# Four mixed layers on one core: GpSimd's share of the products with C, whose engine copies a bank, and where loads are issued

## The chip, the cores and the metric

The kernel runs on one core of a Trainium2 chip. A core has five engines with instruction queues of their own: TensorE (PE, with its weight loads shown as PEld), VectorE (DVE), ScalarE (ACT), GpSimd (POOL) and SyncE (SP), which here only issues transfers. Transfers run on 16 DMA engines. The metric is the device time of one execution in microseconds, the median of several runs; smaller is better.

## The reference

Eight images of 96 channels and 64 x 64 pixels pass through four layers, each with a residual and a group norm in front (32 groups of 3 channels):

```python
x = x + _L0_conv_ref(_gn(x), ...)   # selective scan over the 4096 pixels of an image
x = x + _L1_conv_ref(_gn(x), ...)   # Fourier layer
x = x + _L2_conv_ref(_gn(x), ...)   # sampled positions, then 4 scans over patches of 4 x 4
x = x + _L3_conv_ref(_gn(x), ...)   # deformable 3 x 3 convolution
```

The scans of the layers 0 and 2 are, for 192 channels d and 16 states n,

```python
hst = hst * jnp.exp(dt[..., None] * A) + (dt * ut)[..., None] * bt
y = jnp.einsum('bkdn,bkn->bkd', hst, ct)
```

Layer 1 takes a 2-D real Fourier transform of each image, gates it by a grouped 24 x 24 product with gelu and a soft threshold, transforms back, projects the channels, and normalises with the mean and variance over all eight images before a last gelu. So nothing of its end can be finished before the last image has been transformed. All is float32.

## The kernel before, in words

**Scans.** Layers 0 and 2 work in chunks of 512 pixels. A chunk's 192 channels are 12 groups of 16 channels x 8 states on 128 partitions, with two halves of the states side by side. `Slots` writes the order of work out by hand: in slot t (one group) each engine's queue gets the pieces of several groups at different stages. For a group at slot t these are: at t-4 SP loads `dd` (delta and delta times u, each repeated for 8 states: 512 KB); at t-2 POOL multiplies with B (L348, `dbu`); at t-1 ACT takes the exponentials into PSUM (L327, `ps_d`); at t DVE scans (L675 in layer 0, L1501 in layer 2) and, if the group is not `late`, multiplies with C (L358, two instructions); PE sums over the states (L366). If the group is `late`, the scan writes to SBUF, and POOL does the product with C in one instruction a slot later (L353). In layer 0 the third of each six groups is late, two a chunk, whatever the chunk. `dd` has 5 buffers, `dbu` 6, and each of the two PSUM tiles `ps_d` 2.

Other pieces are put into the same slots with `sl.at(slot, engine, function)`. Layer 0 has 12 slots a chunk and 96 an image (B0 is an image's first slot); the next image's `xn` comes in eight pieces (L535), one a slot from B0 - 84 on, its statistics at B0 - 74 + c (L541). POOL also has the sums of softplus and two gating products (L414 to L426, L722). Layer 2 has 48 slots a chunk (B); a chunk's input rows `xl` are loaded at B - 92 (L1185), normalised at B - 89 on ACT (L1190, `pad`), convolved on PE (L1213), sampled on POOL (L1292 to L1316).

**Layer 1.** Per image: `down` (12 banks: two products on PE, L808, then four copies of 64 x 256 into `tr`), `along` (L833, evicted on ACT, L837), `gate` (L858 to L865, ACT and DVE), statistics of the image before on DVE (L936), four `down` of the next image, `project` (L875, evicted on ACT as `pt`, L882, 13 copies), then twelve `back` (L894) with the other eight `down` and six `up` (L913) between them. The order is written out, too. All products use one rotation of eight PSUM banks. In `down` the copies of a bank go alternately to DVE (L822, partitions 0 to 63 of `tr`) and ACT (L824, the others).

**The seam.** After the last image `yr` is read back, its statistics are taken, and the scale and shift of the normalisation computed (L976 to L983). `between()` sets up the weights of layer 2 (`weights2`: loads, products on PE, L1084 to L1113). Then four images are finished here: load `x` (L993), gelu on `yr` (ACT, L1015), addition (DVE, L995), store (L996), statistics (L229). The other four are finished in 16 pieces inside layer 2 (loads L1011 and L1012, addition L1672, statistics L1674, store L1020), 5, 5 and 6 of them in three batches, loaded at the slots -92, -60 and -46. Here the order is left to a scheduler, but for the slots of layer 2. The buffers of the finishing `x`, and layer 2's pools, lie in memory that earlier pools held, and become free when these pools are done. SP issues its transfers in order, and waits in this order for buffers and data.

Of the kernel before, what the change touches and what calls it, by code (L numbers as in the profile page):

```python
# [18 lines left out]
CH = 96  # L19
# [475 lines left out]
def layer0(S, src, dst, st_in, st_out, images):  # L495
    tc, nc = S.tc, S.nc
    with ExitStack() as ctx:
# [27 lines left out]
        def image(b, B0):  # L525
            im = {}

            def load():
                im["xn"] = xn = new(fp, [CH, 3 + NP], "xn", bufs=2)
                nc.vector.memset(xn[:, 0:3], 0.0)  # L530
                im["bns"] = new(fp, [CH, NC, 6], "ibns", bufs=2)

            def piece(c):
                at = slice(3 + c * NW, 3 + (c + 1) * NW)
                return lambda: nc.sync.dma_start(  # L535
                    im["xn"][:, at], src[b][:, c * NW : (c + 1) * NW]
                )

            def stats(c):
                def run():  # L540
                    nc.vector.bn_stats(  # L541
                        im["bns"][:, c, :], im["xn"][:, 3 + c * NW : 3 + (c + 1) * NW]
                    )

                return run

            im["nm"] = new(fp, [CH, 1], f"nm{b}")
            def normal(c):
                def run():
                    x = im["xn"][:, 3 + c * NW : 3 + (c + 1) * NW]  # L550
                    nc.scalar.activation(
                        x, x, AF.Identity, bias=im["nm"], scale=st_in[:, b, 1:2]
                    )

                return run

            sl.at(B0 - 84, "sp", load)
            for c in range(NC):
                sl.at(B0 - 84 + c, "sp", piece(c))
                sl.at(B0 - 74 + c, "dve", stats(c))  # L560
            GroupStats(
                S, sl, B0 - 62, st_in[:, b, :], lambda: im["bns"], fp, psk, "ps_k", im["nm"]
            )
            for c, t in enumerate((-50, -49, -46, -45, -38, -37, -34, -33)):
                sl.at(B0 + t, "act", normal(c))
            im["obns"] = new(fp, [CH, NC, 6], f"obns{b}")
            return im

        def chunk(im, b, c, T):
# [103 lines left out]
            def scan_of(n):  # L673
                def scan(i, out, da, dbu):
                    nc.vector.tensor_tensor_scan(  # L675
                        out, da, dbu, carry[:, n + i : n + i + 1] if c else 0.0, ALU.mult, ALU.add
                    )

                return scan
# [8 lines left out]
            def y_of(h, g):  # L688
                def run():
                    if g == 0:  # L690
                        ch["y", h] = new(psy, [128, NW], "ps_y")
                    return ch["y", h][:HD, :], g == 0, g == NG - 1

                return run
# [15 lines left out]
            for h in range(2):  # L710
                for g in range(NG):
                    t, n = T + h * NG + g, 2 * (h * NG + g)
                    sl.groups[t] = Group(
                        n=g, a=acol[:, n : n + 2], steps=steps_of(h, g), b=lambda: ch["b"],
                        c=lambda: ch["c"], y=y_of(h, g), scan=scan_of(n), late=g == 2,
                    )
                    if c < NC - 1:
                        sl.at(t, "end", keep(t, n))
                sl.at(T + (h + 1) * NG + 1, "dve", skip(h))
# [46 lines left out]
def layer1(S, src, mid, dst, st_in, st_out, images, finish, between):  # L766
# [4 lines left out]
    with ExitStack() as ctx:  # L771
# [17 lines left out]
        with ctx1:  # L789
# [10 lines left out]
            def down(im, q):  # L800


                if q == 0:
                    im["tr"] = new(ip, [128, IH, CH], "tr")
                ps = ps_of()
                for r in range(2):
                    c0 = 4 * q + 2 * r
                    nc.tensor.matmul(  # L808
                        ps[:, r * 256 : (r + 1) * 256],
                        im["xh"][:, c0 : c0 + 2, :].rearrange("h c w -> h (c w)"),  # L810
                        fh,
                        start=True,
                        stop=True,
                    )
                to = im["tr"].rearrange("p k (s q r i) -> p q i r s k", s=2, r=2, i=2)
                for i in range(2):
                    for part in range(2):
                        o = to[part * 64 : part * 64 + 64, q, i]
                        v = ps[i * 64 : i * 64 + 64, :]
                        v = v.rearrange("p (r s q k) -> p q r s k", r=2, s=2, q=2)[:, part]  # L820
                        if part == 0:
                            nc.vector.tensor_copy(o, v)  # L822
                        else:
                            nc.scalar.copy(o, v)  # L824
# [156 lines left out]
        nc.vector.tensor_tensor(mv[:, 0:1], mv[:, 0:1], vec[:, 0:1], ALU.subtract)  # L981
        nc.vector.tensor_tensor(sc[:, 1:2], mv[:, 0:1], sc[:, 0:1], ALU.mult)
        nc.vector.tensor_tensor(sc[:, 1:2], vec[:, 2:3], sc[:, 1:2], ALU.subtract)  # L983
        between()
        with ExitStack() as ctx2:
            ip = ctx2.enter_context(tc.tile_pool(name="l1j", bufs=3))
            psp = ctx2.enter_context(tc.tile_pool(name="l1g", bufs=2, space=PSUM))

            here = list(kept)[-4:]
            for b in here:  # L990
                yb = kept[b]
                xb = new(ip, [CH, NP], "x2")
                nc.sync.dma_start(xb, src[b])  # L993
                finish.gelu(yb)
                nc.vector.tensor_tensor(xb, xb, yb, ALU.add)  # L995
                nc.sync.dma_start(dst[b], xb)  # L996
                S.image_stats(st_out[:, b, :], xb, wp, psp, "ps")
# [30 lines left out]
def weights2(S, cp):  # L1028

    tc, nc = S.tc, S.nc  # L1030
    with tc.tile_pool(name="l2s", bufs=4, space=PSUM) as psa:
# [34 lines left out]
        centre = new(cp, [HD, 2, HD], "centre")  # L1066
        nc.vector.tensor_tensor(centre[:, 0, :], S.ident[:HD, :HD], kmean, ALU.subtract)
        nc.vector.tensor_scalar(centre[:, 1, :], kmean, -1.0, None, ALU.mult)
        with tc.tile_pool(name="l2t", bufs=1) as tp:
            wx = S.load("l2_wx", tp)  # L1070
            off1 = S.load("l2_off1", tp).rearrange("e h k o -> e h (k o)")
            xp = S.load("l2_xp", tp)
            dtw = S.load("l2_dt", tp)
            ds = new(tp, [CH, 4, DI], "ds")
            nc.sync.dma_start(ds, S.ins["l2_d"].unsqueeze(0).to_broadcast([CH, 4, DI]))
            nc.vector.tensor_tensor(ds[:, 0:2], ds[:, 0:2], ds[:, 2:4], ALU.add)
            nc.vector.tensor_tensor(wds, ds[:, 0], ds[:, 1], ALU.add)
            nc.vector.tensor_tensor(wds, wds, win[:, :DI], ALU.mult)
            flat = woff.rearrange("c k o -> c (k o)")
            for n in range(4):  # L1080
                at = slice(432 * n, 432 * n + 432)
                ps = ps_of()
                for h in range(2):
                    nc.tensor.matmul(  # L1084
                        ps[:CH, :432], wx[:, h, :], off1[:, h, at], start=h == 0, stop=h == 1
                    )
                nc.scalar.copy(flat[:, at], ps[:CH, :432])
            xpm = new(tp, [CH, 1, 4 * (RK + 2 * NS)], "xpm")
            ps = ps_of()
            for h in range(2):  # L1090
                nc.tensor.matmul(
                    ps[:CH, : 4 * 38],
                    wx[:, h, :],
                    xp[:, h].rearrange("e k c -> e (k c)"),
                    start=h == 0,
                    stop=h == 1,
                )
            nc.vector.tensor_copy(xpm[:, 0, :], ps[:CH, : 4 * 38])
            for k in range(4):
                at = 38 * k + RK  # L1100
                for what in range(2):
                    replicate(
                        nc, rep_w[:, k, what], xpm[:, 0, at + what * NS : at + (what + 1) * NS]
                    )
                ps = ps_of()
                for h in range(2):
                    nc.tensor.matmul(
                        ps[:RK, :CH], xp[:, h, k, :RK], wx[:, h, :], start=h == 0, stop=h == 1
                    )
                low = new(tp, [RK, CH], f"low{k}")  # L1110
                nc.vector.tensor_copy(low, ps[:RK, :CH])
                ps = ps_of()
                nc.tensor.matmul(ps[:CH, :DI], low, dtw[:RK, k, :], start=True, stop=True)  # L1113
                m = ORDER.index(k)
                nc.vector.tensor_copy(wd[:CH, m, :], ps[:CH, :DI])
                nc.sync.dma_start(wd[CH : CH + 1, m], S.ins["l2_dt"][RK : RK + 1, k])
# [6 lines left out]
def layer2(S, src, dst, st_in, st_out, images, cp, W, ready, finish):  # L1123
# [3 lines left out]
    with ExitStack() as ctx:  # L1127
# [8 lines left out]
            )  # L1136
        )

        fp = ctx.enter_context(tc.tile_pool(name="l2f", bufs=1))
        wp = ctx.enter_context(tc.tile_pool(name="l2w", bufs=1))  # L1140
        sl = Slots(S, cp, wp, psd)
        log_exp_tables(S)
        acol = sl.negative_exp("l2_alog")
# [33 lines left out]
        def front(ch, b, pad, xs, c, B):  # L1177
# [21 lines left out]
                r = 0 if c == 0 else 9  # L1199
                nc.gpsimd.memset(pad[:, r, :], 0.0)  # L1200

            sl.at(B - 92, "sp", load)
            sl.at(B - 89, "act", normal)
            if c in (0, NC - 1):
                sl.at(B - 89, "pool", border)
# [945 lines left out]
```

## Time and profile before

| | |
|---|---|
| median of 3 timed runs | 17438.37 us (17433.97 to 17443.99) |
| the profiled execution | 18287.47 us, its span 18285.7 us, mean granted clock 0.900 |
| busy share of the span | PE 78%, PEld 29%, DVE 89%, ACT 56%, POOL 84% |
| first scan instructions of layer 2 | 3961.71 us |
| last scan product of layer 2 | about 14454 us |
| HBM read and written | 579.53 MB and 87.69 MB |

The profiled execution is some 850 us longer than the timed ones, so a time from the trace is compared with other times of the trace. In the page, the busy share of an engine counts instructions that compute; a line of the groups gives the line in the kernel, engine, operation, output and inputs with their shapes, the count, the summed busy time, the mean duration in ns, and after the second bar the idle time just ahead of them with what ended it. A timeline row has start and length in us, and in brackets the idle time before it and its releaser. A row of the chain of waits has start, length and what was waited for or worked on. The windows view gives busy time per engine in stretches of the span.

### The profile page before, as it was taken

The page shows a single profiled execution, that of the slowest core. Times are in us where ns is not written, and L with a number is a line of the kernel's source. Part 1 is how long each engine was busy: PE and PEld are TensorE (multiplying, and loading weights), DVE is VectorE, ACT ScalarE, POOL GpSimd, SP SyncE. Part 2 cuts the span into 40 slices and gives each one's busy share as a digit, 9 for nine tenths or more (in the row PEclk, how much of TensorE's full clock was granted, in tenths as well). Part 3 has the DMA queues.
Part 4 walks back from the last instruction along what each step waited for, and adds up shares of the span by engine and source line. Part 5 has one row for each costly group of instructions (what it writes and reads, how often), then busy time and mean ns, then how long its engine had stood idle before and what let it go on. Part 6 is the DMA issues. An engine that isn't in the chain of part 4 may idle for free.

```text
span 18285.7 us, 141860 instructions
## 1 busy us (share of the span) xinstructions
PE 14310.8 (78%) x34756; PEld 5304.7 (29%) x34756; DVE 16268.6 (89%) x16810; ACT 10307.5 (56%) x17016; POOL 15303.1 (84%) x9100
## 2 busy tenths in 40 slices
PE   8999998858888888898898988889888644434333
PEld 2323334723333333333333333333333211111111
DVE  7999997559999999999999999999999766767667
ACT  6777775546666666766666666676666411111100
POOL 7999995049999999999999999999999656656555
PEclk8999998879999999999999999999999866666666
DMA  7888886269999999999999999999999745444444
GB/s 128 151 153 151 151 151 107 56 139 157 158 158 158 158 158 157 159 157 158 158 157 159 157 159 158 158 158 158 158 157 158 139 127 152 143 136 144 135 129 120
DMA packets 941060, 2689.99 MB, mean 147 GB/s; under 512 B 274482, under 2 KB 276223, under 8 KB 938605
## 3 DMA queue, kind: packets, MB, share of 16 engines
q1 hardware_dynamic: 792781, 2227.79, 70.0%
q0 software_dynamic: 147456, 453.13, 8.4%
q8 instruction: 284, 4.65, 0.1%
q14 instruction: 539, 4.42, 0.1%
HBM read 579.53 MB, written 87.69 MB: 36 GB/s over the span
## 4 chain that ended last, share of the span: by engine, by line
POOL 21%; PE 21%; issue 20%; DVE 18%; another core or an unknown queue 11%; ACT 5%; DMA 4%; SPq 0%; POOLq 0%; DVEq 0%; ACTq 0%
POOL dbu L348 12%; PE ps_y L366 9%; DVE ps_d L1501 7%; DVE dbu L358 6%; DMA dd<-delta 3%; POOL dbu L353 2%; PE ps_k L577 2%; PE ps_a L1820 2%; POOL sp_m L1435 1%; POOL delta L1443 1%; PE ps_o L2054 1%; DVE ps_d L675 1%; POOL sp_w L1438 1%; PE ps_k L1213 1%
## 5 line engine op out<-in xcount | busy, mean ns | idle before, releaser
L348 POOL TENSOR_TENSOR dbu<-dd,brep 128x1024 f32<-128x1024 f32 x3840 | 9062.4, 2376 | 187.8 <-DMA dd<-delta 127.2
L366 PE MATMUL ps_y<-dbu,k_red 128*96 128x512 f32 x15360 | 7447.2, 612 | 817.3 <-DVE dbu L358 496.5
L1501 DVE TENSOR_TENSOR_SCAN ps_d<-ps_d,dbu 128x512 f32<-128x512 f32 x5760 | 6710.3, 1208 | 83.7 <-POOL dbu L348 68.9
L327 ACT ACTIVATE ps_d<-dd,l_alog 128x512 f32<-128x512 f32 x7680 | 4991.7, 681 | 2708.3 <-DVE dbu L358 2571.5
L358 DVE TENSOR_TENSOR dbu<-ps_d,crep 128x512 f32<-128x512 f32 x7040 | 4437.1, 668 | 0.0
L366 PEld LDWEIGHTS ps_y<-dbu,k_red 128*96 128x96 f32 x15360 | 2407.3, 166 | 5459.1 <-issue 3158.6
L1985 POOL DMA_INDIRECT v<-t,idx x2304 | 2185.7, 949 | 1570.1 <-DVE s L2012 730.7
L2012 DVE TENSOR_REDUCE s<-v 128x864 f32<-128x3456 f32 x256 | 1554.2, 6071 | 369.7 <-remote 314.9
L2003 DVE TENSOR_TENSOR v<-v,ps_w 128x3456 f32<-128x3456 f32 x256 | 958.4, 3744 | 735.3 <-ACT ps_w L1995 658.4
L675 DVE TENSOR_TENSOR_SCAN ps_d<-ps_d,carry,dbu 128x512 f32<-128x512 f32 x1120 | 1373.4, 1271 | 80.9 <-POOL dbu L348 50.5
L2031 ACT COPY smp<-ps_t 128x768 f32<-128x768 f32 (+1 forms) x512 | 244.4, 529 | 1793.3 <-remote 1197.4
L1213 PE MATMUL ps_k<-pad,woff 96*96 96x512 f32 x2304 | 1093.8, 597 | 69.4 <-ACT pad L1190 66.9
L1480 PE MATMUL ps_a<-xs,rep_w 96*128 96x512 f32 x2048 | 1097.9, 617 | 53.3 <-ACT brep L1488 51.9
L2023 PE MATMUL ps_t<-k_ident,s 128*128 128x128 f32 (+1 forms) x1792 | 328.3, 334 | 1014.8 <-issue 695.1
L353 POOL TENSOR_TENSOR dbu<-h,crep 128x1024 f32<-128x1024 f32 x320 | 755.7, 2362 | 126.1 <-DVE h L1501 126.1
L1820 PE MATMUL ps_a<-xpad,l_om 96*27 96x512 f32 x1152 | 594.7, 667 | 22.5 <-issue 22.5
L1837 PE MATMUL ps_u<-k_ident,oc 27*128 27x27 f32 x256 | 33.0, 252 | 740.0 <-ACT oc L1832 666.8
L2023 PEld LDWEIGHTS ps_t<-k_ident,s 128*128 128x128 f32 (+1 forms) x1792 | 251.6, 170 | 1149.0 <-issue 985.1
L1213 PEld LDWEIGHTS ps_k<-pad,woff 96*96 96x96 f32 x2304 | 372.1, 164 | 708.9 <-issue 583.1
L1162 POOL MEMSET pad<- 96x660 f32 x4 | 2.4, 648 | 683.1 <-DMA y<-yb 683.1
L1435 POOL TENSOR_TENSOR sp_m<-sp_m,sp_s 128x512 f32<-128x512 f32 x384 | 495.4, 1290 | 59.1 <-ACT sp_s L1423 59.1
L1480 PEld LDWEIGHTS ps_a<-xs,rep_w 96*128 96x128 f32 x2048 | 347.1, 189 | 665.0 <-ACT brep L1488 286.2
(268 smaller groups left out, 17180.5 us busy)
## 6 DMA issues: line engine op xcount, KB each, us to landing
dd<-delta SPq DMA_DIRECT2D x3840, 512.0 KB
v<-t,idx POOLq DMA_INDIRECT x2304
xo<-x SPq DMA_DIRECT2D x128, 192.0 KB
x<-xo SPq DMA_DIRECT2D x128, 192.0 KB
xn<-x SPq DMA_DIRECT2D x64, 192.0 KB
xh<-x SPq DMA_DIRECT2D x16, 768.0 KB
y<-yb SPq DMA_DIRECT2D x16, 768.0 KB
yr<-y SPq DMA_DIRECT2D x8, 1536.0 KB
```

The lines of the kernel that those rows point to most:

```text
L327: nc.scalar.activation(da, g.dd[:, 0, :], AF.Exp, scale=g.a[:, i : i + 1])
L348: nc.gpsimd.tensor_tensor(g.dbu, g.dd[:, 1:2, :].to_broadcast([128, 2, NW]), g.b(), ALU.mult)
L353: nc.gpsimd.tensor_tensor(g.dbu, g.both, g.c(), ALU.mult)
L358: nc.vector.tensor_tensor(g.dbu[:, i, :], g.h[i], g.c()[:, i, :], ALU.mult)
L366: self.S.nc.tensor.matmul(y, self.red[:, 80 - GC * g.n : 176 - GC * g.n], g.dbu[:, i, :], start=first and i == 0, stop=last and i == 1,)
L675: nc.vector.tensor_tensor_scan(out, da, dbu, carry[:, n + i : n + i + 1] if c else 0.0, ALU.mult, ALU.add)
L1213: nc.tensor.matmul(ch["pk"][:HD, :], woff[:, k, m * HD : (m + 1) * HD], pad[:, dy : dy + 8, dx : dx + IW], start=k == 0, stop=k == KT - 1,)
L1480: nc.tensor.matmul(dr["pa"], rep_w[:, k, what, s, :], xs[:CH, k % 2, :], start=True, stop=True,)
L1501: nc.vector.tensor_tensor_scan(out[:, way], da[:, way], dbu[:, way], 0.0, ALU.mult, ALU.add)
L1820: nc.tensor.matmul(im["pa"][: 3 * KT, :], om[:, k, :], xpad[:, 8 * c + dy : 8 * c + dy + 8, dx : dx + IW], start=k == 0, stop=k == KT - 1,)
L1985: nc.gpsimd.indirect_dma_start(out=st["v"][:, k].rearrange("p q c -> p (q c)"), out_offset=None, in_=flat, in_offset=bass.IndirectOffsetOn ...
L2012: nc.vector.tensor_reduce(st["s"], st["v"].rearrange("p k q c -> p k c q"), mybir.AxisListType.X, ALU.add,)
```

## The change

- Layer 0: the third group of a chunk's second half is late in even chunks only. In odd chunks DVE does that product, so POOL has one product with C there and two in even chunks.
- Layer 0: an image's `xn` pieces are issued every second slot from B0 - 90 to B0 - 76.
- Layer 1: all four copies of an even bank of `down` are done by DVE, those of an odd bank by ACT.
- The seam: the first three loads of `x` are issued before `between()`, the fourth in the loop as before; their pool waits per tile for what lay in its memory. The temporary weights' pool `l2t` is put on the right side of the memory.
- Layer 2: its two working pools wait per tile; `xl` is loaded at B - 100 instead of B - 92.

```diff
-            sl.at(B0 - 84, "sp", load)
+            sl.at(B0 - 90, "sp", load)
             for c in range(NC):
-                sl.at(B0 - 84 + c, "sp", piece(c))
+                sl.at(B0 - 90 + 2 * c, "sp", piece(c))
                 sl.at(B0 - 74 + c, "dve", stats(c))
...
-                        c=lambda: ch["c"], y=y_of(h, g), scan=scan_of(n), late=g == 2,
+                        c=lambda: ch["c"], y=y_of(h, g), scan=scan_of(n),
+                        late=g == 2 and (h == 0 or c % 2 == 0),
...
-                        if part == 0:
+
+                        if q % 2 == 0:
                             nc.vector.tensor_copy(o, v)
                         else:
                             nc.scalar.copy(o, v)
...
-        between()
         with ExitStack() as ctx2:
-            ip = ctx2.enter_context(tc.tile_pool(name="l1j", bufs=3))
+            ip = ctx2.enter_context(tc.tile_pool(name="l1j", bufs=3, reuse_waits="tile"))
             psp = ctx2.enter_context(tc.tile_pool(name="l1g", bufs=2, space=PSUM))
 
             here = list(kept)[-4:]
+            x = {}
+
+            def load(b):
+                x[b] = new(ip, [CH, NP], "x2")
+                nc.sync.dma_start(x[b], src[b])
+
+            for b in here[:3]:
+                load(b)
+            between()
             for b in here:
-                yb = kept[b]
-                xb = new(ip, [CH, NP], "x2")
-                nc.sync.dma_start(xb, src[b])
+                if b not in x:
+                    load(b)
+                yb, xb = kept[b], x[b]
                 finish.gelu(yb)
...
-        with tc.tile_pool(name="l2t", bufs=1) as tp:
+        with tc.tile_pool(name="l2t", bufs=1, side="right") as tp:
...
-        fp = ctx.enter_context(tc.tile_pool(name="l2f", bufs=1))
-        wp = ctx.enter_context(tc.tile_pool(name="l2w", bufs=1))
+        fp = ctx.enter_context(tc.tile_pool(name="l2f", bufs=1, reuse_waits="tile"))
+        wp = ctx.enter_context(tc.tile_pool(name="l2w", bufs=1, reuse_waits="tile"))
...
-            sl.at(B - 92, "sp", load)
+            sl.at(B - 100, "sp", load)
             sl.at(B - 89, "act", normal)
```

## The prediction

> **What bounds the kernel now.** I read the page (busy shares, slices) first, cut the span into its layers with the windows view, then read groups, timeline and the chain of waits in each.
>
> ```profile
> DVE  7999997559999999999999999999999766767667
> POOL 7999995049999999999999999999999656656555
> ```
>
> The dip in slices 7 to 9 is the Fourier layer and the seam behind it; left of it lies the first layer (to about 3010 us), right of it the third (3960 to 14450 us), then the fourth. The windows view of one stretch in each of the first three:
>
> ```profile
> 1371.00:1828.00 457.00, 429.07 (x904) 138.43 (x902) 438.95 (x497) 343.39 (x688) 445.25 (x196) 0.96 0.89 151
> 3070.00:3630.00 560.00, 492.76 (x3017) 395.81 (x3016) 314.40 (x561) 286.21 (x454) 0.00 (x0) 0.84 0.25 49
> 4113.00:4570.00 457.00, 409.90 (x919) 144.55 (x917) 454.34 (x526) 316.05 (x491) 446.28 (x244) 0.99 0.93 157
> ```
>
> Columns: length, busy time of PE, weight load, DVE, ACT, POOL, clock, DMA share, GB/s. In the first layer POOL is at 445.25/457 = 97.4% and DVE at 96.1%: POOL leads, DVE is close. In the third DVE (99.4%) leads. In the Fourier layer nobody is full: a chain. The groups of the first layer, 600 to 2400 us:
>
> ```profile
> L348 POOL TENSOR_TENSOR dbu<-dd,brep 128x1024 f32<-128x1024 f32 x474 | 1105.5, 2352 | 46.9 <-DMA dd<-delta 34.3 <-PE ps_y L366 4.4 <-DVE ps_d L675 4.2
> L675 DVE TENSOR_TENSOR_SCAN ps_d<-ps_d,carry,dbu 128x512 f32<-128x512 f32 x689 | 845.1, 1271 | 54.5 <-POOL dbu L348 35.1 <-ACT ps_d L327 17.0 <-ACT sp_m L388 2.1
> L358 DVE TENSOR_TENSOR dbu<-ps_d,crep 128x512 f32<-128x512 f32 x790 | 500.0, 673 | 0.0
> ```
>
> 474 groups in 1800 us at 12 a chunk are 39.5 chunks of 45.57 us. The Fourier layer between two images, timeline:
>
> ```profile
> 3582.24 4.83 DVE L936 BATCH_NORM_STATS2 bns<-yr 96x6 f32<-96x512 f32 x8
> 3586.99 0.56 DVE L822 COPY tr<-ps 64x256 f32<-64x256 f32 x1
> 3587.64 0.58 ACT L824 COPY tr<-ps 64x256 f32<-64x256 f32 x1 [9.06 <-DVE tr L822]
> 3588.25 1.19 DVE L822 COPY tr<-ps 64x256 f32<-64x256 f32 x2 [0.70 <-ACT tr L824]
> ...
> 3594.43 0.58 ACT L824 COPY tr<-ps 64x256 f32<-64x256 f32 x1 [0.66 <-DVE tr L822]
> ```
>
> DVE and ACT take turns, one idle while the other copies, and ACT can't begin before DVE has done its statistics; ACT's 13 copies `pt` (L882, 10.54 us) start at 3595.04 only. The seam, from the chain of waits:
>
> ```profile
> 3736.79 9.17 DMA x<-x
> ...
> 3770.36 13.82 DMA x<-x
> ...
> 3788.66 7.05 DMA x<-x
> ...
> 3803.23 11.77 DMA xl<-x
> ...
> 3881.31 11.27 DMA xl<-x
> ```
>
> Here transfers end the waits while the engines stand: ACT idles 26.85 us before the second `xl` (3892.60).
>
> **What the skill says.** The Trainium skill, "GPSIMD Engine Reference", section 4.1, calls GpSimd about 2x slower than VectorE for two inputs; the trace has 2352 ns against 2 x 673, a factor 1.75. "SBUF — State Buffer", section "Who interferes with whom": a VectorE instruction with at most one SBUF input outside the 2-port modes doesn't contend with GpSimd; L358 reads one operand in PSUM, and L348 spreads only from 2330 to 2507 ns (median 2363), so more products on DVE shouldn't slow POOL. "PSUM — Partial Sum Buffer", section "PSUM bank collisions raise a hardware error": accesses of two engines to one bank and quadrant are kept apart by a dependency; the trace shows it, ACT waits 138 times, 164.1 us, for L822. "DMA: Bandwidth & Descriptors", section "Queues, rings and completion order": each DMA engine consumes a ring in order; the first `xl`, issued behind ten 384 KB loads, landed 11.8 us after issue.
>
> **First layer.** The third product of the second half goes from POOL to DVE in odd chunks: 4 of 8 chunks an image, 32 in all. Mean per chunk: POOL 44.4 us (445.25/457 x 45.57) less 2.352/2 = 43.2; DVE 43.8 plus half a pair of products. A pair moves the next scan by 1.19 us in the timeline (two records of 673 overlap), so 44.4. Before the four scan groups of that view DVE idled 71.3 us, 38 of it for POOL and 29 for ACT: 0.97 and 0.73 a chunk. POOL's part goes, since POOL gets slack on average; ACT's stays: 44.4 + 0.73 = 45.1, a gain of 0.4, times 64 = 26 us. Bounds: 0 (another wait fills it) and 45.57 - 44.4 = 1.17 a chunk, 75 us. The even chunks keep POOL at 44.4, so alternate chunks must average through the buffers two groups deep; 1 us is within that. The wait that decides next is DVE for ACT's exponentials after the silu with its two table loads.
>
> The `xn` loads come every second group instead of every group, and end two slots before their statistics. POOL's 34.3 us behind `dd` cluster at these bursts (5.2 us in 1900 to 2100, none in 1000 to 1200). A group moves 512 KB in 3.8 us; a 192 KB piece each group makes 185 GB/s, every second one 160, against 151 at 89% share. This relief is inside the 26, not added.
>
> **Fourier layer.** Each bank is copied four times by one engine. In the changed kernel's instruction order these copies wait for PE alone, so the turns do end. First image: 12 banks took 3033.75 to 3056.6 in turns, 48 copies; two engines with 6 banks each need 24 x 0.59 = 14.2 and start 1 us apart: 7.6 us less. Between images, four banks precede `pt`: ACT's two banks no longer wait for DVE; ACT is free at 3578.6, PE's last bank is there at 3580.9, so ACT ends at 3583.4 instead of 3595.0. Then `pt` needs banks: eight rotate, the fifth `pt` product takes the first bank, which DVE copies after its statistics (3587.0 + 2.4). So four `pt` copies run early, the fifth ends about 3591.4, the seventh waits for DVE's second bank (3591.8), the thirteenth ends about 3599.2 against 3605.6: 6.4 us an image, 7 images with a successor: 45. Bounds: 3 us (banks are late more often) and 9.6 (no bank late). In the later eight banks PE issues without a break, some 2.6 us a step against 2.5 for the turns, so there I count nothing. Sum 53 (29 to 75).
>
> **Seam.** Reference times are those of the profile. Now the first three `x` loads wait until the weights' tiles are free (3736.8). Changed: they queue right behind `yr` (landed 3712.65). Price of one 1.5 MB transfer: 13.82 us for a store and a load, so 6.9: they land at 3719.5, 3726.4 and 3733.3. The first gelu ends at 3725.0, so the first addition comes at 3725 instead of 3746. Behind it stand the weights' loads: `off1` (1.3 MB, 5.8 us) lands near 3740 instead of 3720, its products (16 records, 8.74) end at 3749, DVE's rest (6.8, mixed with statistics) near 3762 instead of 3737. DVE: two additions (4.4 each) to 3734, two statistics and small weights to 3746, third addition 3750.5. The fourth load reuses the first buffer, so it stands behind three stores' issue; with three transfers ahead and itself it lands at about 3771, addition to 3776, against 3788.6. The first `xl` is now issued right there, ahead of the ten pieces, and no longer after the whole pool (7.05 us store, then the pieces): behind one store it lands near 3785 against 3815.1. Gain 30. The weights (3762) are in time for it; they would decide from 23 us later. The pieces land by about 3802; their gelus stand behind the first convolution, so they delay it by little.
>
> The second `xl` is ahead of the last piece loads instead of behind twelve of them: ACT's 26.85 us go, 27. What is late next is the convolution itself (11 us) and the pieces' gelus. Sum 57 (30 to 80). Per-tile waits for buffers are part of these numbers; `l2t` on the right side costs no instruction.
>
> **Third layer, steady.** `xl` (240 KB) moves eight groups up, next to the 192 KB store. DMA is at 93%. Before, POOL waited 64.6 us for `dd` in 108 waits over 4200 to 14400 us, 1 us a chunk. Cost taken: 0, since each group is loaded four ahead; bounds -10 and +40.
>
> **Sum.** 26 + 53 + 57 = 136. Against its own run, 18287.5 us (span 18285.7), that is 18151. The timed runs have 17438.4, 849 less than the profiled one; where the profile adds, I can't see, so I take the 136 at full size: **17302 us**.
>
> **Rivals.** (1) The loads that jump ahead only push the weights back, and the first convolution waits for these: the seam gives 15, 26 + 53 + 15 = 94, 17344. For: FIFO behind 4.5 MB. Against: 23 us of margin. (2) DVE takes over the first layer's bound at once: 0 there, 110 in all, 17328. For: DVE at 96%. Against: half its idle is POOL's. (3) Slower: the third layer's `xl` and the store fall together, `dd` comes late where POOL has 2.34 + 1.25 us of work in a 3.55 us group, and DVE, at 99.4%, inherits it. From 136/64 = 2.1 us a chunk this decides; at 3 us it is 192 - 136 = 56 slower, 17494. For: DMA 93%. Against: present waits are 0.6 us each. (4) The chain of DVE gates and PE sets the Fourier layer anyway, and the seam's gain is lost in POOL's later start: about 10 us, no change.
>
> **Chances.** Forecast 0.67, (1) 0.11, (2) 0.09, (3) 0.08, (4) 0.05. The forecast's own range is 17235 to 17375 (205 and 63 gained: the parts' ends don't meet). The range takes in (1), (2) and a small cost in the third layer: 17230 to 17400. A change of 0.2% (35 us) is what a measurement can tell: faster 0.87, same 0.05, slower 0.08.
>
> **What would show it.** First layer: POOL below 96%, DVE above 97%, chunks near 45.1 us, waits for `dd` at image starts gone. Fourier: L822's and L824's waits for each other gone, about 74 us an image instead of 80.5. Seam: first addition near 3725 less the gains ahead, ACT's two waits for `xl` under 5 us together. Third layer: waits for `dd` still about 65 us. Wrong if the third layer lengthens by over 60 us, or if weights end the first convolution's wait.

## The result, and the profile after

The changed kernel takes **17354.98 us** (five runs, 17353.6 to 17361.88) against 17438.37 (17433.97 to 17443.99): ratio 0.9952, 95% interval 0.9940 to 0.9964, 83 us or 0.48% less. The forecast was 17302, 136 less. The kernel is faster, and its time lies within the range of the forecast, but one part went the other way (times from the traces, in us):

| stage | before | after | difference | forecast |
|---|---|---|---|---|
| first layer, start of its last scan (L675) | 3005.5 | 3047.5 | +42.0 | -26 |
| to the first bank copy (L822; L824 after) | 28.2 | 27.2 | -1.0 | 0 |
| Fourier layer, to the last `yb` copy | 659.1 | 589.3 | -69.8 | -53 |
| seam, to layer 2's first scan | 268.9 | 207.6 | -61.3 | -57 |
| third layer, first to last scan (L1501; L1511 after) | 10490.8 | 10491.6 | +0.8 | 0 |

The sum is -89. The fourth layer isn't compared: it takes 3833 us in the trace of before and 2990 in that of after. This difference is nearly all of the 849 us which the prediction left unexplained, and it goes with the chip and not with the change. On the chip of the first four experiments below the fourth layer takes 3790 to 3824 us with every kernel, and the kernel before 18265.24 us in all; on the two chips of the other eight it takes 2990 to 2995 us, and the kernel before 17446.08 and 17441.29. What differs is not known: GpSimd's indirect loads (L1985; L1995 after) last 949 ns each in both traces. All stages ahead of it agree between the chips, and I compare these.

The page after, and the windows view of stretches in the first, the Fourier and the third layer (the columns as in the prediction):

```profile
DVE  7999999659999999999999999999999997988888
...
POOL 7999999019999999999999999999999996777777
```

```profile
1371.00:1828.00 457.00, 426.51 (x885) 137.01 (x884) 436.80 (x498) 335.13 (x669) 429.27 (x189) 0.94 0.89 150
3110.00:3630.00 520.00, 473.44 (x3169) 377.32 (x3169) 334.41 (x593) 298.83 (x472) 0.00 (x0) 0.91 0.30 58
4023.00:4480.00 457.00, 410.24 (x918) 145.02 (x917) 453.98 (x526) 316.15 (x491) 445.82 (x245) 0.99 0.93 157
```

In the first layer POOL fell from 445.25 to 429.27 us, as it should; but DVE, with more products to do, did less in the same time, too (438.95 to 436.80). Both wait more than before. The groups of 600 to 2400 us name what they wait for:

```profile
L348 POOL TENSOR_TENSOR dbu<-dd,brep 128x1024 f32<-128x1024 f32 x468 | 1094.3, 2358 | 107.1 <-DMA dd<-delta 86.6 <-PE ps_y L366 9.0 <-PE ps_a L658 4.2
...
L675 DVE TENSOR_TENSOR_SCAN ps_d<-ps_d,carry,dbu 128x512 f32<-128x512 f32 x718 | 880.8, 1271 | 62.2 <-POOL dbu L348 45.4 <-ACT ps_d L327 14.8 <-ACT carry L684 1.1
L327 ACT ACTIVATE ps_d<-dd,l_alog 128x512 f32<-128x512 f32 x936 | 609.1, 682 | 95.9 <-DMA dd<-delta 71.6 <-DVE h L675 18.5 <-DVE dbu L358 3.7
L358 DVE TENSOR_TENSOR dbu<-ps_d,crep 128x512 f32<-128x512 f32 x816 | 516.2, 673 | 0.0
```

POOL's waits for `dd` went from 34.3 to 86.6 us, and 468 groups instead of 474 fit into the stretch. L348's mean is 2358 ns (2352 before), with 816 of DVE's products L358 in the stretch where there were 790. The Trainium skill, "SBUF — State Buffer", section "Who interferes with whom", has a VectorE instruction with at most one SBUF input, outside the 2-port modes, not contend with GpSimd; the traces agree.

The Fourier layer between two images, timeline after:

```profile
3274.14 4.95 ACT L826 COPY tr<-ps 64x256 f32<-64x256 f32 x8 [1.93 <-PE ps L809]
...
3275.87 4.83 DVE L938 BATCH_NORM_STATS2 bns<-yr 96x6 f32<-96x512 f32 x8
3279.11 10.72 ACT L884 COPY pt<-ps 66x480 f32<-66x480 f32 x13
3280.63 5.03 DVE L824 COPY tr<-ps 64x256 f32<-64x256 f32 x8
```

ACT copies its two banks at once, and its 13 `pt` copies follow without a gap; they begin while DVE is still at its statistics. The seam, chain of waits after (start, length):

```profile
3664.01 0.70 DVE yb L924
...
3736.86 4.43 DVE x L1005
3741.31 0.33 SPq L1006
3741.68 0.43 SPq L1195
3742.20 1.91 SPq L1021
3744.16 10.86 DMA dd<-x
3755.03 9.19 DMA dd<-x
3764.25 1.28 ACT L1025
```

The first `xl` (SPq L1195) is now issued ahead of the pieces (L1021; their loads are the rows `dd<-x`). No transfer of `xl` is left in the chain; those of the pieces and ACT's gelus on them (L1025) are.

### The profile page after: what moved, and what is told of

It reads as the page before. It is cut to its first block, busy times and chain, and to the rows that moved or that the text cites. A ratio compares the mean times of both kernels' runs of the same rounds, so it can differ in the third digit from the quotient of the medians.

```text
span 17353.1 us, 141873 instructions
## 1 busy us (share of the span) xinstructions
PE 14371.3 (83%) x34756; PEld 5326.6 (31%) x34756; DVE 16322.5 (94%) x16874; ACT 10314.5 (59%) x17016; POOL 15231.2 (88%) x9068
## 4 chain that ended last, share of the span: by engine, by line
POOL 31%; issue 23%; DVE 17%; PE 17%; DMA 7%; ACT 4%; SPq 0%; POOLq 0%; DVEq 0%; ACTq 0%
POOL v L1995 12%; POOL dbu L348 11%; PE ps_y L366 8%; DVE ps_d L1511 8%; DMA dd<-delta 6%; DVE dbu L358 6%; POOL dbu L353 2%; PE ps_k L577 2%; DVE ps_d L675 1%; ACT ps_d L327 1%; POOL sp_m L1445 1%; POOL delta L1453 1%; POOL delta L1461 1%; POOL sp_w L1448 1%; PE ps_a L621 1%
## 5 line engine op out<-in xcount | busy, mean ns | idle before, releaser
L348 POOL TENSOR_TENSOR dbu<-dd,brep 128x1024 f32<-128x1024 f32 x3840 | 9034.5, 2365 | 291.5 <-DMA dd<-delta 222.4
L1511 DVE TENSOR_TENSOR_SCAN ps_d<-ps_d,dbu 128x512 f32<-128x512 f32 x5760 | 6712.6, 1209 | 83.6 <-POOL dbu L348 69.0
L358 DVE TENSOR_TENSOR dbu<-ps_d,crep 128x512 f32<-128x512 f32 x7104 | 4487.9, 671 | 0.0
L1995 POOL DMA_INDIRECT v<-t,idx x2304 | 2185.9, 949 | 752.1 <-issue 694.3
L2022 DVE TENSOR_REDUCE s<-v 128x864 f32<-128x3456 f32 x256 | 1549.2, 6051 | 27.2 <-DVE v L2013 1.4
L675 DVE TENSOR_TENSOR_SCAN ps_d<-ps_d,carry,dbu 128x512 f32<-128x512 f32 x1184 | 1452.5, 1271 | 92.4 <-POOL dbu L348 67.9
L2033 PE MATMUL ps_t<-k_ident,s 128*128 128x128 f32 (+1 forms) x1792 | 364.5, 367 | 1358.9 <-DVE s L2022 1358.8
L353 POOL TENSOR_TENSOR dbu<-h,crep 128x1024 f32<-128x1024 f32 x288 | 678.9, 2357 | 127.5 <-DVE h L1511 127.4
L1445 POOL TENSOR_TENSOR sp_m<-sp_m,sp_s 128x512 f32<-128x512 f32 x384 | 490.3, 1277 | 32.2 <-ACT sp_s L1433 32.2
L577 PE MATMUL ps_k<-xn,wk 96*96 96x512 f32 x1024 | 501.0, 613 | 3.1 <-ACT xn L551 2.4
```

Source lines behind the costliest of these rows:

```text
L348: nc.gpsimd.tensor_tensor(g.dbu, g.dd[:, 1:2, :].to_broadcast([128, 2, NW]), g.b(), ALU.mult)
L353: nc.gpsimd.tensor_tensor(g.dbu, g.both, g.c(), ALU.mult)
L358: nc.vector.tensor_tensor(g.dbu[:, i, :], g.h[i], g.c()[:, i, :], ALU.mult)
L675: nc.vector.tensor_tensor_scan(out, da, dbu, carry[:, n + i : n + i + 1] if c else 0.0, ALU.mult, ALU.add)
L1511: nc.vector.tensor_tensor_scan(out[:, way], da[:, way], dbu[:, way], 0.0, ALU.mult, ALU.add)
L1995: nc.gpsimd.indirect_dma_start(out=st["v"][:, k].rearrange("p q c -> p (q c)"), out_offset=None, in_=flat, in_offset=bass.IndirectOffsetOn ...
```

## The experiments

Twelve kernels were run. All have the changed Fourier layer but none of them is the changed kernel; b_copy has nothing else of the change, s_x and s_xl92 take back one part of the changed seam each, and the other nine have the whole of it. The table gives the stages as above (us), and the whole time as a ratio to the kernel before on the same chip:

| kernel | first layer's last scan | Fourier | seam | third | median | ratio, 95% interval |
|---|---|---|---|---|---|---|
| a_burst | 3012.0 | 588.3 | 207.7 | 10495.5 | 18162.85 | 0.9945 (0.9925 to 0.9965) |
| a_late | 3043.5 | 587.2 | 207.8 | 10492.0 | 18184.24 | 0.9957 (0.9941 to 0.9973) |
| a_first | 3001.6 | 588.7 | 207.7 | 10491.2 | 18137.40 | 0.9935 (0.9916 to 0.9954) |
| b_copy | 3007.2 | 587.3 | 263.8 | 10493.3 | 18193.50 | 0.9965 (0.9952 to 0.9979) |
| d_dense | 2992.3 | 587.0 | 207.6 | 10491.4 | 17303.60 | 0.9921 (0.9904 to 0.9937) |
| d_four | 3029.2 | 592.8 | 205.3 | 10492.4 | 17342.25 | 0.9940 (0.9924 to 0.9957) |
| d_ahead | 2985.4 | 588.4 | 207.7 | 10492.6 | 17298.75 | 0.9917 (0.9901 to 0.9934) |
| d_ahead_spread | 3010.8 | 587.6 | 207.6 | 10492.7 | 17324.28 | 0.9932 (0.9916 to 0.9949) |
| e_best | 2983.8 | 587.9 | 207.8 | 10491.2 | 17292.97 | 0.9915 (0.9898 to 0.9931) |
| e_best_late | 2992.1 | 588.1 | 207.6 | 10491.5 | 17300.71 | 0.9918 (0.9902 to 0.9935) |
| s_x | 3002.0 | 587.8 | 207.7 | 10491.2 | 17312.23 | 0.9924 (0.9908 to 0.9941) |
| s_xl92 | 3007.2 | 589.4 | 248.6 | 10490.1 | 17351.28 | 0.9947 (0.9930 to 0.9963) |

The stages are sharper than the whole times: the five traces with the first layer as before (before, a_first, b_copy, s_x, s_xl92) have its last scan at 3001.6 to 3007.2, and waits of POOL for `dd` of 28.0 to 37.5 us between 600 and 2400 us. Differences of less than these spreads tell nothing.

**Which edit of the first layer costs.** Theory S blames the spread of the loads, rival L the moved product. a_burst takes back the first, a_late the second, a_first both:

```diff
-            sl.at(B0 - 90, "sp", load)
+            sl.at(B0 - 84, "sp", load)
-                sl.at(B0 - 90 + 2 * c, "sp", piece(c))
+                sl.at(B0 - 84 + c, "sp", piece(c))
```

> The changed kernel with the image loads of the first layer as they were (from B0 - 84, one piece a group); the third product stays in turns on DVE and GpSimd. Theory S (the spread of the loads costs: the queue is overfull for 16 groups instead of 8, and dd comes late): the first layer's last scan starts 42 to 68 us earlier than the changed kernel's 3047.5, time 17287 to 17313, and POOL's waits for dd between 600 and 2400 us fall from 86.6 to some 35 us. Rival L (the product moved to DVE costs): no change, 17345 to 17365, waits as they were.

```diff
-                        late=g == 2 and (h == 0 or c % 2 == 0),
+                        late=g == 2,
```

> The changed kernel with the third product of the second half always on GpSimd, as before; the loads stay spread. Theory S: no gain, 17355 to 17381 (26 slower if the moved product is worth what was predicted), waits of POOL for dd stay above 60 us. Rival L: about 42 us faster, 17313, first layer's last scan near 3005.

> The changed kernel with the whole first layer as before: what the Fourier layer, the seam and the third layer give without it. All theories: 42 us faster than the changed kernel (the stage's own difference between the two traces), 17313, that is 125 under the kernel before; first layer's last scan near 3005. A time near 17355 would say that the longer first layer of the changed kernel's trace is not the edit's doing.

Against the mean of the five, 3004.7, the last scan comes 39 us later with the spread alone (a_late), 7 later with the moved product alone (a_burst) and 43 later with both (after). S holds and L falls. Three numbers of S were missed: a_burst, at 3012.0, isn't as early as S with a gain of 26 asked for, and its waits for `dd` are 48.4 us, not 35; those of a_late are 52.6 us, not above 60. The moved product gains nothing here.

**How the spread costs.** There are two theories. P: each piece makes the `dd` load behind it late, so what counts is how many `dd` loads have a piece ahead. R: the rate is over what the queue carries. The base is a_first; the pieces are put into two groups (slots) with four each, or into every fourth group:

```diff
-                sl.at(B0 - 84 + c, "sp", piece(c))
+                sl.at(B0 - 80 + c // 4, "sp", piece(c))      # d_dense, with load at B0 - 80
+                sl.at(B0 - 106 + 4 * c, "sp", piece(c))      # d_four, with load at B0 - 106
```

> First layer of before (third product as before), but the eight image pieces in two groups of four (B0 - 80 and B0 - 79) instead of one a group; Fourier layer and seam as changed. Base of comparison: the same kernel with one piece a group, whose first layer's last scan starts at 3001.6. Theory P (each piece that stands ahead of a dd load makes that one late, because a dd load lands about 10 us after its issue and has little to spare; what counts is how many dd loads have a piece ahead): the same or earlier, 2985 to 3004. Rival R (the rate counts: what is over the queue's 150 to 160 GB/s piles up): the pile is 10 us at once, so later than 3001.6, 3005 to 3040.

> The same base, the pieces every fourth group (from B0 - 106, 32 groups). Theory P: as bad as every second group or worse, last scan of the first layer at 3038 or later, POOL's waits for dd between 600 and 2400 us above 50 us. Rival R: about 160 GB/s is what the queue can carry, so no pile: 3001 or earlier, waits below 28 us.

Both go against R, and with pieces up to every second group the denser is the better: 2992.3 with the pieces in two groups, 3001.6 in eight, 3043.5 spread over 16. The 32 groups of d_four give 3029.2, 9 us better than P asked, but 28 behind the burst, with 52.4 us of waits for `dd`. The waits view of POOL, 600 to 2400 us (us in all, times, longest), of a_first:

```profile
POOL dbu L348 <- DMA dd<-delta: 28.0, 20, 4.2
```

and of a_late, where only the spread is added:

```profile
POOL dbu L348 <- DMA dd<-delta: 52.6, 38, 2.8
```

A wait is 1.4 us on average in both: the spread makes more of them, not longer ones. Where a piece may get in the way is seen at SP, which issues in order. These are the pieces' issues on SP in a_first (count; shortest, median, longest in ns; first and last start),

```profile
L535 SPq DMA_DIRECT2D xn<-x x64: 423/587/4417, 6.5 to 2359.0; - x64
```

and these in a_late and in d_four:

```profile
L535 SPq DMA_DIRECT2D xn<-x x64: 424/4074/4440, 6.5 to 2405.9; - x64
```

```profile
L535 SPq DMA_DIRECT2D xn<-x x64: 312/2662/4500, 6.5 to 2387.3; - x64
```

The issue itself holds SP for 4.1 us in the median where the pieces are spread over every second group, longer than the 3.8 us that a group lasts, and SP's next `dd` stands behind it; it is 2.7 us in d_four, 0.6 in the burst, and 0.46 in d_dense. The order is that of the last scans. It is no full account: in the burst the `dd` issues take 4.2 us instead, as in these rows of SP's timeline of a_first.

```profile
2342.15 0.60 SPq L535 DMA_DIRECT2D xn<-x  x1
2342.85 4.20 SPq L319 DMA_DIRECT2D dd<-delta  x1
2347.09 0.59 SPq L535 DMA_DIRECT2D xn<-x  x1
```

One piece and one `dd`, 704 KB, go out every 4.94 us there, which is 146 GB/s (an estimate from these rows), about the 152 that the queue moves on average in 600 to 2400 us. So a long issue may be no cause, but only the sign of a full queue; no run tells the two apart. Nor does one move the pieces to other slots at the same density, so their place isn't ruled out as a part of the cause.

If `dd` loads are late because they have too little to spare, a sixth buffer and a load five groups ahead must help:

```diff
-        g = G(t + AHEAD)
+        g = G(t + self.ahead)            # 5 in layer 0, 4 in layer 2
-            g.dd = new(self.pool, [128, 2, NW], "dd", bufs=AHEAD + 1)
+            g.dd = new(self.pool, [128, 2, NW], "dd", bufs=self.ahead + 1)
```

> The same base (one piece a group), but the first layer loads dd five groups ahead with six buffers instead of four and five. Theory P: one group more (3.8 us) to spare takes nearly all waits for dd away: POOL's waits between 600 and 2400 us from 28 to under 6 us, last scan 15 to 45 us earlier, 2957 to 2987. Rival R: the pile of a burst is 10 us, 3.8 more to spare takes a part: 2985 to 3000.

> The changed kernel whole (pieces every second group, third product in turns) with dd five groups ahead and six buffers in the first layer. Theory P: the spread's 36 to 39 us go, last scan near 2960 to 3000 instead of 3047.5. Rival R: the queue stays overfull for 16 groups, one group more to spare is used up early: 3030 or later. It also tells what the third product in turns is worth once dd is in time: against the run with dd five ahead and the third product as before, 26 us less by the prediction, 5 to 10 more if DVE is the bound.

On the base the waits fall to 3.7 us and the layer by 16. The last scan, 2985.4, lies in the ranges of both theories; the waits are P's. On the changed kernel it comes 37 us earlier, at 3010.8, between the two theories: 40.8 us of waits are left. So P has the direction, but one group more to spare isn't enough for the spread, whose pieces still hold SP for 4.03 us each in the median. What makes an issue long isn't settled.

**What the moved product is worth with `dd` in time.** The kernel e_best joins dense pieces and five ahead (both diffs above); e_best_late adds the moved product.

> The changed kernel's Fourier layer and seam; first layer with the third product as before, image pieces in two groups of four and dd five groups ahead. Theory P: the two gains are the same waits, so they add up only in part: POOL's waits for dd near 0 between 600 and 2400 us, last scan of the first layer 2970 to 2985 (2992.3 with the pieces dense alone, 2985.4 with five ahead alone), time 17283 to 17298. Rival R: dense pieces make the pile 10 us, which one more group cannot hold: 2990 or later.

> The kernel of the label e_best, and with it the third product of the second half in turns as in the changed kernel: the worth of that edit with dd in time. The prediction's step: 26 us less in the first layer. Rival theory (DVE is the bound as soon as it takes the product: it was 4 to 10 us later in the two pairs with dd late): 5 to 15 us more.

The two gains are for the most part the same waits, as P has it: 2983.8 with both, where one alone gave 2992.3 and 2985.4. Groups of e_best, 600 to 2400 us (L349 is the line L348 of before, L676 is L675):

```profile
L349 POOL TENSOR_TENSOR dbu<-dd,brep 128x1024 f32<-128x1024 f32 x478 | 1114.2, 2356 | 0.0
...
L676 DVE TENSOR_TENSOR_SCAN ps_d<-ps_d,carry,dbu 128x512 f32<-128x512 f32 x697 | 855.1, 1272 | 35.7 <-ACT ps_d L328 22.2 <-POOL dbu L349 6.1 <-ACT carry L685 4.1
```

POOL waits for no load any more, and DVE's waits for POOL in this group are 6.1 us where they were 35.1 before, though POOL has all its products. Groups of e_best_late:

```profile
L676 DVE TENSOR_TENSOR_SCAN ps_d<-ps_d,carry,dbu 128x512 f32<-128x512 f32 x736 | 903.0, 1272 | 24.4 <-ACT ps_d L328 12.5 <-POOL dbu L349 11.1
...
L354 POOL TENSOR_TENSOR dbu<-h,crep 128x1024 f32<-128x1024 f32 x59 | 138.9, 2355 | 18.4 <-DVE h L676 18.4
```

Now POOL stands and waits for DVE's scan, DVE is busy for 1754.09 of 1800 us, and the layer is 8.3 us longer, where the prediction's step had 26 less. The next table has the times from one chunk's last statistics to the next chunk's (L740; the rows of `obns` in the timeline), from the third image's first chunk to the fourth image's first, in us:

| chunk to chunk | 1 | 2 | 3 | 4 | 5 | 6 | 7 | 8 | sum |
|---|---|---|---|---|---|---|---|---|---|
| before | 49.1 | 44.7 | 44.6 | 44.6 | 44.6 | 44.2 | 44.5 | 47.0 | 363.3 |
| after | 52.1 | 45.9 | 44.1 | 45.0 | 45.8 | 44.1 | 44.9 | 49.2 | 371.1 |
| e_best | 47.6 | 46.4 | 43.1 | 46.1 | 44.6 | 44.2 | 44.5 | 45.5 | 361.8 |
| e_best_late | 47.6 | 46.3 | 44.1 | 45.0 | 44.1 | 44.6 | 43.9 | 47.1 | 362.6 |

The middle of an image, intervals 2 to 7, is alike in all four, 44.5 to 45.0 us a chunk on average, whoever does the product. What differs is the two ends: interval 8 holds the groups in which the next image's pieces are loaded (the spread has three of them in interval 7), interval 1 DVE's eight statistics of them (L541, 0.68 us each). There the spread costs and the clump with five ahead gains. Why the product gains nothing in the middle can be read from a stretch of it, first of before, then of e_best_late:

```profile
1050.00:1230.00 180.00, 170.30 (x358) 54.31 (x357) 173.21 (x196) 134.13 (x258) 179.49 (x79) 0.96 0.89 152
1050.00:1230.00 180.00, 170.10 (x357) 54.68 (x357) 175.90 (x201) 134.34 (x258) 173.55 (x76) 0.96 0.89 151
```

Before, POOL is full there (179.49 of 180 us), yet DVE has no wait for POOL in it: the 6.5 us of DVE's waits are for ACT (5.2) and PE (1.3). The moved product takes 5.9 us from POOL and gives 2.7 to DVE, whose waits shrink to 3.7 us. DVE's work and its waits for ACT and PE fill the stretch in both kernels.

**Fourier layer alone.** This edit is made to the kernel before:

```diff
-                        if part == 0:
+                        if q % 2 == 0:
```

> The kernel before with only the bank copies changed (each bank by one engine). If the stage of the changed trace is the edit's alone: 69.8 us faster than before, 17368; from the Fourier stage 591 us instead of 661. By the prediction's sum 53: 17385. Rival (half of the stage's gain comes from the other edits): 17400 or more.

The stage takes 587.3 us instead of 659.1: its whole gain is this edit's, and the seam is 5.1 shorter besides. By the whole times the edit is worth 72 us, with an interval from 38 to 88. The Trainium skill, "PSUM — Partial Sum Buffer", section "PSUM bank collisions raise a hardware error", says why the turns were there: accesses of two engines to one bank and quadrant get a dependency. The traces agree: with one engine a bank, L824 and L826 of the changed kernel wait for no engine but PE (100.3 and 67.1 us), and ACT's 164.1 us behind DVE are gone.

**The seam.** From a_first, one part is taken back at a time: the loads of `x` and their pool,

```diff
-            for b in here[:3]:
-                load(b)
-            between()
+        between()      # ahead of the pool l1j, which waits as a whole
...
+                nc.sync.dma_start(xb, src[b])
```

> The kernel of the label a_first with the x loads between the layers where they were (behind the weights, three buffers, waits of the whole pool); the third layer's loads and its per-tile waits as changed. The prediction's 30 us are the x loads' (first addition 3725 instead of 3746, everything behind it earlier): by it the seam gets 20 to 30 us longer than 207.7, 228 to 238. Rival theory: the gain is the per-tile waits of the third layer's pools and the earlier xl: under 10 us longer.

or the place of `xl`:

```diff
-            sl.at(B - 100, "sp", load)
+            sl.at(B - 92, "sp", load)
```

> The kernel of the label a_first with xl of the third layer at B - 92 as before. By the prediction's 27 us (second xl behind twelve piece loads): seam 235 or so instead of 207.7; third layer's scans 10491 as ever (cost taken: 0). Rival theory: with the first xl in time and the pieces issued earlier the second xl is hidden anyway: seam under 215.

The loads of `x` are worth nothing: the seam takes 207.7 us either way. The place of `xl` is worth 40.9: 248.6 us without it, where 235 was expected. The chain of s_xl92 has `xl` twice, each time behind the pieces (`dbu<-y`), as before the change:

```profile
3705.67 12.40 DMA dbu<-y
3718.09 10.37 DMA xl<-x
...
3783.55 9.97 DMA dbu<-y
3793.58 11.21 DMA xl<-x
```

The chain of s_x, weights first:

```profile
3620.15 0.70 DVE yb L924
...
3640.38 7.55 DMA l_xp<-l_xp
...
3661.88 4.33 DVE x L997
```

Counted from the last `yb` copy, its `x` loads are issued from 27.3 us on and its first addition comes at 41.7, against 44.0 and 53.3 before the change and 11.0 and 32.1 after it. Yet its fourth addition ends at 78.7 and the first `pad` starts at 88.2; after the change these are 77.3 and 87.6. The loads that jump ahead change places with the weights: `l_wx`, the large `l_off` and `l_xp` are issued at 13.4, 13.8 and 20.2 us in s_x, but after the change at 26.9, 33.6 and 40.4, each as one of the three `x` loads lands. And the fourth `x` load, which takes a buffer over from a stored `x`, goes out at 56.3 and at 57.6 us, so it hardly gains from the head start. That the first three are issued 16.7 us earlier in s_x than before, although `between()` stands first again, fits with their not waiting for the weights' tiles any more: before, this wait ended with a product of the weights (L1113), in s_x with the landing of the weights' loads. The edit that is left for this is the weights' pool on the other side of the memory. It and the per-tile waits share the last 15.2 us (263.8 to 248.6), if the parts add up; neither was tried alone.

## Why the prediction was right or wrong

- **First layer: wrong in sign**, +42 for -26, by two steps. The loads' spread "is inside the 26, not added": it was reckoned as a relief from mean rates (185 and 160 GB/s; with the 1024 bytes that a KB has in these views it is 190 and 164), and costs 36 to 39. DMA share and rate are 0.89 and about 150 GB/s with it and without; what tells is how often a `dd` load is late. And "POOL's part goes, since POOL gets slack": DVE's 0.97 us a chunk behind POOL wasn't from POOL's own work in the middle of an image (the stretch shown above has no such wait), but mostly from `dd` come late to POOL at the images' ends. With POOL's work as before, e_best leaves 9.3 of these 38.4 us (600 to 2400 us), while DVE's waits for ACT grow from 28.6 to 36.7; it has 45.2 us a chunk (361.8/8), about the 45.1 that the prediction had from the moved product. That product itself makes the layer 4, 7 and 8 us longer in the three pairs of traces (the 4 is within their spread): it is DVE's work that decides, the mechanism of rival (2), which counted it as 0.
- **Fourier layer: right mechanism, term too small**, 69.8 for 53. The mutual waits went, and an image takes 71.8 us instead of 81.4 (means of the six steps between the statistics of seven images: 3175.25 to 3663.63 before, 3203.78 to 3634.76 after); the prediction read 80.5 for before and expected 74. The term is the 6.4 us an image: it had the fifth `pt` product wait for a bank that DVE copies late. No such wait came: over all images PE's products L877 stood 0.4 us behind DVE and ACT's copies L884 0.5 us behind PE. The gain of 9.6 is the forecast's own bound for no late bank. The first image's 12 banks gave 6.9 for 7.6 (22.8 us before; 15.9 after, 3074.75 to 3090.6).
- **Seam: right size, wrong shares**, 61.3 for 57, so that the size is luck in part. The first addition came where it was expected, 32.1 us behind the last `yb` copy (3725 is 32.2), and so did the price, the large `l_off` 47.3 us behind it (3740 is 47.2); but of "gain 30" the loads of `x` have 0. Rival (1), where these loads only push the weights back, had this right; its seam of 15 was too small, since the gain comes from elsewhere. The place of `xl` gives 40.9, of which some 16 come with its first transfer and 25 with its second (27 forecast); the rest is 15.2 for pools and 5.1 from `down`. ACT still waits 14.9 us for the first `xl`, not under 5, but the chain then goes through the pieces' loads, which land later.
- **Third layer: right.** +0.8; POOL's waits for `dd` from 4200 to 14300 us are 59.8 us (59.2 before). With `xl` back at B - 92 it is 10490.1.
- **The whole**: the forecast was 68 us too good in the first layer and 21 too bad in the next two stages, which leaves 47 of the 53 us by which it was off; 6 are between the traces and the timed runs. That the time still lies in the range is owed in part to these errors' opposite signs and to the range's width: a loss in the first layer was outside the bounds set for that part.

The fastest version is e_best, 17292.97 us, 0.9915 of before (0.9898 to 0.9931): the first layer with its old products, loads in two clumps and `dd` five ahead, the rest as changed. By the whole times it can't be told from d_ahead (0.9917), which has no clumps.

## What to carry to other kernels

Take the time of each round and not a mean over rounds: where most run alike and a few are long, the long ones hold the loss, and a wait "for POOL" there can be a wait for the load that POOL waits for. Where a stream of loads comes just in time, try other loads in a clump, or one buffer more for the stream, before you spread them thin. Ahead of a chain of weights and data, ask of each load which of the two ends last before you move it up.

## What the runs showed of the hardware

Eight pieces of 192 KB an image, spread over 16 groups (a_late), make the first layer 39 us longer over eight images than one a group, and in a clump of two groups (d_dense) 12 us shorter, at a DMA share of 0.88 to 0.89 in each. An issue on SP isn't always short: one of `dd` (L319) takes 545 ns in the median but up to 4839 in the trace after, so a load written into the list isn't yet one on its way. And three chips gave the same times for three layers (a_first and s_x: 10491.2 us both for the third), but on one of them the fourth took some 3800 us where it took 2990 on the other two.
